# A graph layer on one core: four of 1024 gathers become single row loads, messages are formed in place, edges get four buffers

## The chip, the cores and the metric

The kernel runs on one core of a Trainium2 chip. The metric is device time in microseconds of one execution; the kernel before has a median of 1315.23 us over three runs (1314.40 to 1316.04).

## What is computed

One layer of a graph network on 8192 nodes with 256 channels and 131072 edges, sorted by target, all in float32. Cut to what matters:

```
msg  = relu(x[src] + edge_attr @ w_e + b_e)          # 131072 x 256; edge_attr has 64 columns
t    = x + segment_sum(msg, dst)                     # 8192 x 256
h1   = bn(relu(t @ w1 + b1) @ w2 + b2 + x)           # local branch
h2   = bn(attention(x) @ out_w.T + out_b + x)        # 4 heads within groups of 32 nodes
o    = h1 + h2
o    = bn(o + relu(o @ m_w1 + m_b1) @ m_w2 + m_b2)
out  = layernorm(x + o)
```

## The kernel before

**Tiles.** The edges are cut into 128 blocks of 1024 (`NB`), each with eight gathers of 128 rows: four groups `h` times two tiles `j`. The nodes are cut into 16 chunks of 512. `x + b_e` is written once to a DRAM tensor `xb`; blocks from 20 (`NX`) on gather from it.

**A block's way.** `gather` (L200) issues eight indirect DMAs on POOL (GpSimd) that bring the rows of `x` into a tile `xs`, of which there are four. `load_edges` (L217) brings a block's edge features with four DMAs on SP (SyncE) into `ea`, two buffers; `edge_transpose` (L237) turns them on DVE (VectorE) into `eaT`. `edge_products` (L245) multiplies them with `w_e` on PE (TensorE) into a pair of PSUM banks `pe`, two buffers, which the attention's scores (`pe<-qk` in the profile) use too. `edge_messages` (L269) adds `pe` and `xs` on DVE into a tile `msg`, three buffers, two instructions a block (L281), and applies relu on ACT (ScalarE, L285). `group_sums` (L300) sums messages by target: eight matmuls of a one-hot tile `oh` with `msg` into `pw`, in four column groups of 32. `edge_place` (L335) puts the sums into the node chunk `xT`.

**Node work.** Attention and the dense layers run as generators in pieces of about 1 to 3 us of PE (`Work`, L783). The program asks for so many microseconds of pieces between the steps of two blocks; behind each piece, and behind each call of `edge_messages`, it calls `between` (L233), which runs the functions in the list `spots`.

**Order.** PE runs in the order in which the code is written. Blocks go in pairs up to 104 (`TAIL`), then singly by a planned clock. From block 24 (`NV`) on, DVE and ACT get their order from the scheduler; SP has its order from the scheduler all through. POOL issues the gathers in order. `hold_fetches` (L183) lets gather number n wait for the last PE instruction that the plan has at or before n x 1.254 - 10 us.

Of the kernel before, what the change touches and what calls it, by code (L numbers as in the profile page):

```python
# [9 lines left out]
FP = mybir.dt.float32  # L10
I32 = mybir.dt.int32
AF = mybir.ActivationFunctionType
# [24 lines left out]
TN = CH // P  # L37
GT = P // NPG
NX = 20
ND = 2  # L40
NV = 24
TAIL = 104
# [36 lines left out]
def gnn_kernel(ctx: ExitStack, tc: tile.TileContext, x, src, dst, edge_attr, w, out):  # L79
    nc = tc.nc  # L80

    const = ctx.enter_context(tc.tile_pool(name="const", bufs=1))
    dram = ctx.enter_context(tc.tile_pool(name="dram", bufs=1, space=DRAM))


    srcd = const.tile([P, ND * NH, TJ], I32, name="srcd")
    for b in range(ND):
        for m in range(EQ):
# [20 lines left out]
    xb = dram.tile([N, C], FP, name="xb")  # L109
# [17 lines left out]
    r = 0  # L127
    for v in VECS:
        n = w[v].shape[0] // P
# [17 lines left out]
    epool = fast.enter_context(tc.tile_pool(name="edge", bufs=1))  # L147
# [10 lines left out]
    xs_of, fetches, marks, mark_at, setup = {}, [], [], [0.0, 0], [True]  # L158
# [7 lines left out]
    def matmul(ps, *args, **kw):  # L166

        mark(ps, nc.tensor.matmul(ps, *args, **kw).ins)  # L168
# [14 lines left out]
    def hold_fetches():  # L183

        i = 0
        for n, fetch in enumerate(fetches):
            if n:
                tc.add_manual_dep(
                    fetch, fetches[n - 1].name,
                    mybir.DependencyInfo(mybir.DependencyClass.NoSync, mybir.DependencyReason.DATA), reason="in order",  # L190
                )
            while i < len(marks) and marks[i][0] <= n * 1.254 - AHEAD:
                i += 1
            if i:
                tc.add_manual_dep(
                    fetch, marks[i - 1][2].name,
                    mybir.DependencyInfo(mybir.DependencyClass.Sync, mybir.DependencyReason.DATA), reason="hold",
                )

    def gather(b):  # L200
        xs = epool.tile([P, NH, TJ, C], FP, name="xs", tag="xs", bufs=4)
        for h in range(NH):
            for j in range(TJ):
                idx = srcd[:, b * NH + h, j : j + 1] if b < ND else srci[:, b, h * TJ + j : h * TJ + j + 1]
                fetches.append(
                    nc.gpsimd.indirect_dma_start(  # L206
                        out=xs[:, h, j, :],
                        out_offset=None,
                        in_=x if b < NX else xb[:, :],
                        in_offset=bass.IndirectOffsetOnAxis(ap=idx, axis=0),  # L210
                    ).ins
                )
        xs_of[b] = xs

    ea_of = {}

    def load_edges(b):  # L217

        ea = ea_of[b] = epool.tile([P, QR + NH * EQ * ED], FP, name="ea", tag="ea", bufs=2)
        for j in range(TJ):  # L220
            for i in range(ED // QR):
                p0, c0 = j * ED + i * QR, (1 - i) * QR
                nc.sync.dma_start(
                    ea[p0 : p0 + QR, c0 : c0 + NH * EQ * ED].rearrange("r (g d) -> r g d", g=NH),
                    edge_attr[b * BE : (b + 1) * BE, :].rearrange("(g j r m) d -> j r g (m d)", j=TJ, r=QR, m=EQ)[j],
                )
# [4 lines left out]
    eaT_of, spots = {}, []  # L231

    def between():  # L233
        for do in spots:
            do()

    def edge_transpose(b):  # L237
        ea = ea_of.pop(b)
        eaT = eaT_of[b] = epool.tile([P, NH * EQ, QR], FP, name="eaT", tag="eaT", bufs=2)
        nc.vector.transpose(eaT, ea[:, QR:].rearrange("p (g d) -> p g d", d=ED)[:, :, :QR])  # L240


    pe_of, msg_of, oh_of, pw_of, newest = {}, {}, {}, {}, {}

    def edge_products(b, pairs=range(0, NH, 2)):  # L245

        eaT = eaT_of[b].rearrange("p (h m) r -> p h (m r)", h=NH)
        for h in pairs:
            pe = bank2().rearrange("p i (u c) -> p i u c", u=2)
            half = [slice(i * ED, (i + 1) * ED) for i in range(2)]  # L250
            if b < NX:
                for i, rows in enumerate(half):
# [8 lines left out]
            pe_of[b, h] = pe  # L261

    def next_edges(b):
        if b < NB:
            edge_transpose(b)
        if b + 2 < NB:
            load_edges(b + 2)

    def edge_messages(b, pairs=range(0, NH, 2), of_pair=range(2)):  # L269

        xs = xs_of[b]
        if b not in msg_of:
            msg_of[b] = epool.tile([P, NH, TJ, C], FP, name="msg", tag="msg", bufs=3)
        msg = msg_of[b]
        n = 2 if b < NB - 1 else 1
        for h in pairs:
            pe = pe_of[b, h]
            for u in of_pair[::n]:
                hs = slice(h + u, h + u + n)
                for js in [slice(0, TJ)] if n == 2 or h + u < NH - 1 else [slice(j, j + 1) for j in range(TJ)]:  # L280
                    nc.vector.tensor_add(  # L281
                        msg[:, hs, js].rearrange("p u i c -> p i u c"), pe[:, js, u : u + n, :],
                        xs[:, hs, js].rearrange("p u i c -> p i u c"),
                    )
                    nc.scalar.activation(msg[:, hs, js], msg[:, hs, js], AF.Relu)  # L285
        between()
# [74 lines left out]
    with tc.tile_pool(name="setup", bufs=1) as sp:  # L361
# [9 lines left out]
        load_edges(1)  # L371
        nc.sync.dma_start(be, w["b_e"][None, :].to_broadcast([P, C]))
        nc.sync.dma_start(dsti_r, dst.rearrange("(s e) -> s e", s=NB))
        in_r = npool.tile([P, 3 * KC, C], FP, name="in_r", tag="m1")
        out_r = npool.tile([P, KC, C], FP, name="out_r", tag="vn")
        vec_r = npool.tile([nrows, P], FP, name="vec_r", tag="pr")
        for v in VECS:
            r, n = col[v]
# [474 lines left out]
    with tc.manual_schedule(engines={PE}):  # L853
# [137 lines left out]
        t, l, s = came[b - 2] + 20, b - 2, b - 2  # L991
        p, m = [b, 0], [b, 0]
# [10 lines left out]
        while l < NB:  # L1003
# [56 lines left out]
            elif t >= times[2]:  # L1060
                i, k = p
# [17 lines left out]
    with tc.If(wide > 0):  # L1079
        with tc.tile_pool(name="gen", bufs=1) as pool, tc.tile_pool(name="gen_ps", bufs=1, space=PSUM) as ps_pool:  # L1080
# [11 lines left out]
            with tc.For_i(0, E, P * TE) as e0:  # L1092
                ea = pool.tile([P, TE, ED], FP, name="gea")
# [7 lines left out]
                xs = pool.tile([P, TE, C], FP, name="gxs")  # L1101
# [7 lines left out]
                for j in range(TE):  # L1109
# [89 lines left out]
```

## Time and profile before

| | us |
|---|---|
| median of three runs | 1315.23 |
| profiled execution, its own time | 1313.34 |
| span of the profiled execution | 1311.6 |
| PE busy | 1199.5 (91%) |
| POOL busy | 975.3 (74%) |
| DVE busy | 797.8 (61%) |
| ACT busy | 584.5 (45%) |

The profile is one execution; the span goes from its first instruction to its last. Rows of groups read: line, engine, operation, out<-in, count, busy time and mean of one in ns, then the engine's idle time before these instructions and what ended it. Times in a timeline count from the span's start.

### The profile page before, as it was taken

Reading aid. Unit: us, or ns where it says so; the run is one execution under the profiler, and the core shown is the slowest. Engines: PE = TensorE matmul, PEld = TensorE weight load, DVE = VectorE, ACT = ScalarE, POOL = GpSimd, SP = SyncE. Lnnn points to the kernel's source line nnn. Section 1 sums busy time; section 2 is a strip of 40 time slices with the busy share of each in tenths; the row PEclk is TensorE's granted clock in tenths of the full one; section 3 lists DMA queues with packets and bytes.
Section 4 is the critical chain, followed back from the end, with each engine's and each line's share of the span. In section 5 each row is a group of like instructions: output and inputs, shape, how many; then the busy total and the mean of one; then the engine's idle time right before and its main releaser. Section 6 shows DMA issues by size and latency. Waiting matters only on the chain.

```text
span 1311.6 us, 21687 instructions
## 1 busy us (share of the span) xinstructions
PE 1199.5 (91%) x7671; PEld 723.0 (55%) x7671; DVE 797.8 (61%) x1630; ACT 584.5 (45%) x840; POOL 975.3 (74%) x1032
## 2 busy tenths in 40 slices
PE   4998999998979979899898988989989799999997
PEld 3564556565545555555555555555555555556576
DVE  6676856757447465475745746456474665766563
ACT  2443534545435355253543536435363443545343
POOL 7777777777777777777777777777777777777772
PEclk9998999999979989899998998989999899999999
DMA  9999985767667666666676666666666675756552
GB/s 230 297 307 280 293 230 158 201 160 191 157 159 188 163 185 162 161 184 157 186 169 169 171 165 184 158 169 180 160 185 163 174 189 138 201 154 185 152 152 64
DMA packets 148926, 240.38 MB, mean 183 GB/s; under 512 B 27950, under 2 KB 112204, under 8 KB 148044
## 3 DMA queue, kind: packets, MB, share of 16 engines
q0 software_dynamic: 49152, 134.28, 38.6%
q1 hardware_dynamic: 98572, 104.65, 29.5%
q8 instruction: 62, 1.02, 0.3%
q14 instruction: 52, 0.43, 0.1%
q10 hardware_dynamic: 1088, 0.00, 0.0%
HBM read 222.06 MB, written 16.78 MB: 182 GB/s over the span
## 4 chain that ended last, share of the span: by engine, by line
PE 69%; DMA 10%; DVE 9%; issue 5%; POOL 3%; ACT 2%; SPq 0%; DVEq 0%; POOLq 0%; ACTq 0%
PE at L168 36%; PE pe L168 18%; PE pw L168 7%; DMA xs<-xb,srci 7%; PE l L168 5%; POOL xs L206 3%; DVE msg L281 3%; DMA xs<-in_x_dram,srci 2%; PE at L704 1%; DVE bd L578 1%; PE at L655 1%; DMA xn<-in_x_dram 1%; ACT msg L285 1%; DVE eaT L240 1%; ACT pr L558 1%
## 5 line engine op out<-in xcount | busy, mean ns | idle before, releaser
L206 POOL DMA_INDIRECT xs<-xb,srci x864 | 820.0, 949 | 263.2 <-issue 168.1
L285 ACT ACTIVATE msg<-msg 128x1024 f32<-128x1024 f32 (+1 forms) x259 | 270.7, 1046 | 472.1 <-DVE msg L281 471.0
L281 DVE TENSOR_TENSOR msg<-pe,xs 128x1024 f32<-128x1024 f32 (+1 forms) x259 | 310.2, 1207 | 261.7 <-DMA xs<-xb,srci 172.5
L168 PE MATMUL pe<-we,eaT 64*128 64x256 f32 x2048 | 263.7, 393 | 6.5 <-DVE msg L281 6.3
L168 PEld LDWEIGHTS pe<-we,eaT 64*128 64x128 f32 x2048 | 191.4, 189 | 100.9 <-issue 60.3
L206 POOL DMA_INDIRECT xs<-in_x_dram,srci x144 | 137.7, 956 | 43.9 <-issue 29.9
L168 PE MATMUL pw<-msg,oh 128*32 128x256 f32 x2048 | 136.1, 385 | 1.6 <-ACT msg L285 1.4
L168 PE MATMUL at<-xT,inT 128*128 128x512 f32 x256 | 121.0, 599 | 2.1 <-ACT xT L507 1.7
L168 PE MATMUL at<-hA,mw 128*128 128x512 f32 (+1 forms) x256 | 115.2, 576 | 0.0
L293 DVE TENSOR_TENSOR oh<-iota_n,rel 128x128 f32<-128x128 f32 x256 | 62.1, 279 | 79.8 <-PE pw L168 79.3
L168 PE MATMUL at<-m,mw 128*128 128x512 f32 (+1 forms) x256 | 108.9, 570 | 0.0
L240 DVE STREAM_TRANSPOSE eaT<-ea 128x512 f32<-128x512 f32 x128 | 89.5, 699 | 21.9 <-PE pe L168 18.8
L168 PEld LDWEIGHTS pw<-msg,oh 128*32 128x32 f32 x2048 | 55.1, 109 | 82.9 <-issue 36.7
L168 PE MATMUL pe<-qk 64*128 64x128 f32 x512 | 50.1, 357 | 51.3 <-DVE msg L281 51.3
L168 PE MATMUL l<-oh,ws 128*128 128x160 f32 (+4 forms) x512 | 87.5, 312 | 1.5 <-ACT xT L507 1.5
L168 PEld LDWEIGHTS l<-oh,ws 128*128 128x128 f32 x512 | 76.3, 200 | 22.1 <-issue 16.3
L168 PEld LDWEIGHTS at<-xT,inT 128*128 128x128 f32 x256 | 47.0, 190 | 59.8 <-issue 51.2
L168 PEld LDWEIGHTS pe<-qk 64*128 64x128 f32 x512 | 43.5, 255 | 61.0 <-DVE msg L281 58.0
L168 PEld LDWEIGHTS at<-m,mw 128*128 128x128 f32 x256 | 47.0, 190 | 46.5 <-issue 45.3
L168 PEld LDWEIGHTS at<-hA,mw 128*128 128x128 f32 x256 | 46.5, 191 | 44.6 <-issue 39.8
L352 DVE TENSOR_TENSOR xT<-l,xT 128x352 f32<-128x352 f32 (+14 forms) x107 | 42.8, 422 | 42.0 <-PE l L168 41.8
L636 ACT ACTIVATE m<-at,vec 128x512 f32<-128x512 f32 (+1 forms) x64 | 41.9, 657 | 54.6 <-PE at L168 54.5
(153 smaller groups left out, 1284.6 us busy)
## 6 DMA issues: line engine op xcount, KB each, us to landing
ea<-in_edge_attr_dram SPq DMA_DIRECT2D x512, 128.0 KB
xs<-xb,srci POOLq DMA_INDIRECT x864
xn<-in_x_dram SPq DMA_DIRECT2D x16, 512.0 KB
out_dram<-y SPq DMA_DIRECT2D x14, 512.0 KB
xp<-in_x_dram SPq DMA_DIRECT2D x10, 512.0 KB
xb<-xp SPq DMA_DIRECT2D x10, 512.0 KB
xp<-in_x_dram SPq DMA_DIRECT2D x3, 1024.0 KB
xb<-xp SPq DMA_DIRECT2D x3, 1024.0 KB
```

The lines of the kernel that those rows point to most:

```text
L168: mark(ps, nc.tensor.matmul(ps, *args, **kw).ins)
L206: nc.gpsimd.indirect_dma_start(out=xs[:, h, j, :], out_offset=None, in_=x if b < NX else xb[:, :], in_offset=bass.IndirectOffsetOnAxis(ap= ...
L240: nc.vector.transpose(eaT, ea[:, QR:].rearrange("p (g d) -> p g d", d=ED)[:, :, :QR])
L281: nc.vector.tensor_add(msg[:, hs, js].rearrange("p u i c -> p i u c"), pe[:, js, u : u + n, :], xs[:, hs, js].rearrange("p u i c -> p i u c"),
L285: nc.scalar.activation(msg[:, hs, js], msg[:, hs, js], AF.Relu)
L293: nc.vector.tensor_tensor(oh[:, ts], iota_n[:, None, :WN].to_broadcast([P, TB // 2, WN]), rel[:, b, ts, None].to_broadcast([P, TB // 2, WN ...
L352: newest["xT"] = nc.vector.tensor_add(xT, l2[:, :, a - n : z - n], xT).ins
L558: nc.scalar.copy(pr[q, :, 2 * hh : 2 * hh + 2, :].rearrange("p t s k -> p s t k"), two4[q, :, :, q])
L578: nc.vector.transpose(bd[q, :, :, g, :].rearrange("p t h q -> p (t h) q"), pr3[q])
L636: newest["relu"] = nc.scalar.activation(m1[:, o, :], layer(mw1, KC, o, hA), AF.Relu, bias=v_("m_b1", o)).ins
L655: nc.tensor.transpose(ps[:wt, t - t2, k * P : (k + 1) * P], zT[:, k, t * P : t * P + wt], ident)
L704: nc.tensor.matmul(ps[i], wt[:, k, o * P : (o + 1) * P], act[:, k, :], start=(k == 0), stop=(k == nk - 1))
```

## The change

- Blocks 46, 62, 78 and 94 (`FETCHED`) issue seven gathers instead of eight. The 128 rows of the last one are loaded by SP into a tile `xf` (two buffers), one DMA of 1 KB for each row. `row_stream` makes pieces of four rows: one load of four row numbers from `last_src` into SP registers, then four DMAs with a register's address.
- From block 26 (`FROM`) on each block gives leave for two pieces (`RUN`), eight rows; `some_rows`, a new function in `spots`, issues one piece where there is leave. 128 pieces take 64 blocks.
- `ea` has four buffers instead of two. `next_edges` loads two blocks ahead up to its block 24, then three, and four from 26.
- Messages are formed in place: `msg` is the tile `xs`, which has six buffers (`BUFS`).
- In the four blocks the last pair's add is three instructions: both groups' first tiles, then the second tile from `xs`, then the one from `xf`.
- A fetch keeps the number that it would have had, so the holds use the same plan as before.

```diff
+BUFS = 6
+RUN = 2
+FETCHED = [46, 62, 78, 94]
+FROM = 26
...
     def gather(b):
-        xs = epool.tile([P, NH, TJ, C], FP, name="xs", tag="xs", bufs=4)
+        xs = epool.tile([P, NH, TJ, C], FP, name="xs", tag="xs", bufs=BUFS)
         for h in range(NH):
             for j in range(TJ):
+                if b in FETCHED and h * TJ + j == TB - 1:
+                    continue
...
-                fetches.append(
+                fetches.append((
+                    b * TB + h * TJ + j,
...
+    def row_stream():
+
+        for b in FETCHED:
+            xf = xf_of[b] = epool.tile([P, C], FP, name="xf", tag="xf", bufs=2)
+            for r in range(QR):
+                _, rows = nc.values_load_multi_w_load_instructions(
+                    last_src[b : b + 1, r * EQ : (r + 1) * EQ], engines=[mybir.EngineType.SP], min_val=0, max_val=N - 1,
+                    skip_runtime_bounds_check_because="src holds rows of x, as for the gathers",
                 )
+                for m, row in enumerate(rows):
+                    nc.sync.dma_start(xf[m * QR + r : m * QR + r + 1, :], xb[ds(row, 1), :])
+                yield
...
+    def fetch_rows(b):
+        quota[0] += RUN if b >= FROM else 0
+
+    def some_rows():
+        if quota[0]:
+            quota[0] -= 1
+            next(rows_to_come, None)
...
-        ea = ea_of[b] = epool.tile([P, QR + NH * EQ * ED], FP, name="ea", tag="ea", bufs=2)
+        ea = ea_of[b] = epool.tile([P, QR + NH * EQ * ED], FP, name="ea", tag="ea", bufs=4)
...
-        if b + 2 < NB:
-            load_edges(b + 2)
+        ahead = 2 + (b >= 24) + (b >= 26)
+        while loaded[0] < min(b + ahead, NB - 1):
+            loaded[0] += 1
+            load_edges(loaded[0])
+        fetch_rows(b - 2)
...
-            msg_of[b] = epool.tile([P, NH, TJ, C], FP, name="msg", tag="msg", bufs=3)
+            msg_of[b] = xs
...
+                if h + u + n == NH and b in FETCHED:
+                    for us, js, rows in (
+                        (slice(0, 2), slice(0, TJ - 1), xs[:, h:]), (slice(0, 1), slice(TJ - 1, TJ), xs[:, h:]),
+                        (slice(1, 2), slice(TJ - 1, TJ), xf_of[b]),
+                    ):
+                        rows = rows[:, None, None, :] if rows is xf_of[b] else rows[:, us, js].rearrange("p u i c -> p i u c")
+                        nc.vector.tensor_add(
+                            msg[:, h:][:, us, js].rearrange("p u i c -> p i u c"), pe[:, js, us, :], rows
+                        )
+                    nc.scalar.activation(msg[:, hs], msg[:, hs], AF.Relu)
+                    continue
...
+        nc.sync.dma_start(last_src, src.rearrange("(s e) -> s e", s=NB)[:, BE - P :])
...
+        spots.append(some_rows)
```

The order of instructions on PE is the same but for the tile's name; what differs is what they wait for. Here PE's sums of one block in the tail are shown with the semaphores that each row waits for, first before, then in the change (`pw` sums, `oh` one-hot tile, DMASW a gather's semaphore).

```order
L168 MATMUL at<-m_6942,mw_95 128x512 x3
L168 MATMUL pw<-msg,oh 32x256 [waits DVE_49,Activation_49]
L168 MATMUL pw<-msg,oh 32x256
L168 MATMUL pw<-msg,oh 32x256 [waits DVE_49]
L168 MATMUL pw<-msg,oh 32x256 x5
```
```order
L172 MATMUL pw<-xs,oh 32x256 [waits DMASW7_49,Activation_49]
L172 MATMUL pw<-xs,oh 32x256 [waits DMASW1_49]
L172 MATMUL pw<-xs,oh 32x256 [waits DMASW3_49,Activation_49]
L172 MATMUL pw<-xs,oh 32x256 [waits DMASW5_49]
L172 MATMUL pw<-xs,oh 32x256 [waits DMASW0_49]
L172 MATMUL pw<-xs,oh 32x256 [waits DMASW2_49]
L172 MATMUL pw<-xs,oh 32x256 [waits DMASW4_49]
L172 MATMUL pw<-xs,oh 32x256 [waits DMASW6_49]
```

Every matmul of a group now waits for a gather by itself, and each also counts up PE's semaphore by itself instead of one for all eight.

On SP, in the part from block 26 on, before: edge loads (`ea`), a chunk's nodes (`xn`) and an output store.

```order
L223 DMA ea<-in_edge_attr_dram 32x4x256 x32
L359 DMA xn<-in_x_dram 128x4x256
L678 DMA out_dram<-y 128x4x256
L223 DMA ea<-in_edge_attr_dram 32x4x256 x32
L359 DMA xn<-in_x_dram 128x4x256
```

And the change, near one such node load (`TENSOR_LOAD last_src` reads four row numbers, `ISA` works out an address, `xf` is a row):

```order
L259 DMA ea<-in_edge_attr_dram 32x4x256 x4
L411 DMA xn<-in_x_dram 128x4x256
L232 TENSOR_LOAD last_src
L237 ISA
L237 DMA xf<-xb 1x256
L237 ISA
L237 DMA xf<-xb 1x256
L731 DMA out_dram<-y 128x4x256
```

Rows stand between all other transfers of SP, also ahead of and behind the store.

On DVE at block 46, before (`msg` adds, `sm` and `pr` softmax, `bd` its turned weights, `eaT` turned edges):

```order
L281 TENSOR_TENSOR msg<-pe,xs 128x2x2x256
L571 TENSOR_REDUCE sm<-pr 128x16
L281 TENSOR_TENSOR msg<-pe,xs 128x2x2x256
L572 RECIPROCAL sm<-sm 128x16
L240 STREAM_TRANSPOSE eaT<-ea 128x512
L574 TENSOR_TENSOR pr<-pr,sm 128x128 x4
```

And in the change:

```order
L333 TENSOR_TENSOR xs<-pe,xs 128x2x2x256
L624 TENSOR_REDUCE sm<-pr 128x16
L327 TENSOR_TENSOR xs<-pe,xs 128x2x256
L625 RECIPROCAL sm<-sm 128x16
L327 TENSOR_TENSOR xs<-pe,xs 128x256
L627 TENSOR_TENSOR pr<-pr,sm 128x128 x4
L327 TENSOR_TENSOR xs<-pe,xf 128x256
L631 STREAM_TRANSPOSE bd<-pr 32x16x32 x4
L276 STREAM_TRANSPOSE eaT<-ea 128x512
```

The second add is cut in three, with softmax steps between its parts, and the edges of a later block are turned behind them. The other three blocks look alike.

More of the change, by code (lines that the diff above doesn't have):

```diff
@@ L185, in hold_fetches @@
         i = 0
-        for n, fetch in enumerate(fetches):
-            if n:
+        former = None
+        for n, fetch in fetches:
+            if former:
                 tc.add_manual_dep(
-                    fetch, fetches[n - 1].name,
+                    fetch, former.name,
                     mybir.DependencyInfo(mybir.DependencyClass.NoSync, mybir.DependencyReason.DATA), reason="in order",
@@ L193, in hold_fetches @@
                 i += 1
+            former = fetch
             if i:
@@ L210, in gather @@
                         in_offset=bass.IndirectOffsetOnAxis(ap=idx, axis=0),
-                    ).ins
-                )
-        xs_of[b] = xs
+                    ).ins,
+                ))
+        xs_of[b] = xs
+    last_src = const.tile([P, P], I32, name="last_src")
+    xf_of = {}
+    def row_stream():
[5 more added lines that the diff above has]
+                    skip_runtime_bounds_check_because="src holds rows of x, as for the gathers",
+                )
+                for m, row in enumerate(rows):
+                    nc.sync.dma_start(xf[m * QR + r : m * QR + r + 1, :], xb[ds(row, 1), :])
+                yield
+    rows_to_come = row_stream()
+    quota = [0]
+    def fetch_rows(b):
[4 more added lines that the diff above has]
+            next(rows_to_come, None)
     ea_of = {}
     def load_edges(b):
-        ea = ea_of[b] = epool.tile([P, QR + NH * EQ * ED], FP, name="ea", tag="ea", bufs=2)
+        ea = ea_of[b] = epool.tile([P, QR + NH * EQ * ED], FP, name="ea", tag="ea", bufs=4)
         for j in range(TJ):
@@ L261, in edge_products @@
             pe_of[b, h] = pe
+    loaded = [3]
     def next_edges(b):
```

## The prediction

> **What bounds the kernel now.** I read the page first: the span, the busy shares, the group of the gathers and the shares of the chain that ended last.
>
> ```profile
> span 1311.6 us, 21687 instructions
> PE 1199.5 (91%) x7671; PEld 723.0 (55%) x7671; DVE 797.8 (61%) x1630; ACT 584.5 (45%) x840; POOL 975.3 (74%) x1032
> ...
> PE 69%; DMA 10%; DVE 9%; issue 5%; POOL 3%; ACT 2%; SPq 0%; DVEq 0%; POOLq 0%; ACTq 0%
> ...
> L206 POOL DMA_INDIRECT xs<-xb,srci x864 | 820.0, 949 | 263.2 <-issue 168.1
> ```
>
> PE is busiest and carries 69% of the chain, so the first guess is that PE is the bound. POOL looks free for a quarter of the time. The second view corrects this: POOL's timeline, two neighbouring gathers, and the instructions of line 206 with their first and last start.
>
> ```profile
> 607.00 0.95 POOL L206 DMA_INDIRECT xs<-xb,srci  x1 [0.30 <-issue]
> 608.25 0.94 POOL L206 DMA_INDIRECT xs<-xb,srci  x1 [0.30 <-issue]
> ...
> ```
> ```profile
> L206 POOL DMA_INDIRECT xs<-xb,srci x864: 942/946/1442, 207.4 to 1289.4; - x173
> ...
> L206 POOL DMA_INDIRECT xs<-in_x_dram,srcd x16: 942/946/1701, 4.4 to 24.6; - x16
> ```
>
> A gather is 0.95 us busy and 0.30 us pause, 1.25 us from start to start. All 1024 start between 4.4 and 1289.4: 1285.0 / 1023 = 1.256 us each. So POOL issues gathers without a break from beginning to end, and its 26% "idle" is the pause that every gather has. What POOL waits for confirms it:
>
> ```profile
> POOL xs L206 <- issue: 205.0, 665, 2.8
> POOL xs L206 <- PE at L168: 25.3, 83, 0.3
> POOL xs L206 <- DMA xs<-xb,srci: 22.9, 75, 0.3
> ```
>
> The waits on other engines are never over 0.3 us, the same pause: neither a full buffer nor the holds of `hold_fetches` stop it. Now who waits for the gathers? The waits between 1000 and 1080 us, then the group that stands there, over the whole run, and PE's busy time in three stretches.
>
> ```profile
> DVE msg L281 <- DMA xs<-xb,srci: 16.9, 7, 4.1
> ...
> PE pe L168 <- DVE msg L281: 7.0, 2, 3.8
> ```
> ```profile
> L168 PE MATMUL pe<-qk 64*128 64x128 f32 x512 | 50.1, 357 | 51.3 <-DVE msg L281 51.3
> ```
> ```profile
> 1025.00:1034.50 9.50, 2.45 (x21) 1.92 (x19) 2.56 (x3) 1.13 (x2) 7.37 (x8) 0.69 0.59 154
> ...
> 1085.00:1217.00 132.00, 129.08 (x828) 77.62 (x832) 85.46 (x172) 63.89 (x98) 100.01 (x106) 0.99 0.64 169
> ```
> ```profile
> 1120.00:1290.00 170.00, 167.35 (x1098) 105.73 (x1097) 109.00 (x236) 79.75 (x128) 128.87 (x136) 1.00 0.62 166
> ```
>
> In a stretch's row the first number behind the length is PE's busy time. Around 1030 PE stands for 7.0 us, because the add that frees its bank waits for a gather: up to there the gathers set the pace and PE follows. The score matmuls (`pe<-qk`) stand like this for 51.3 us in all. Behind that PE is busy 129.1 of 132 us and 167.4 of 170 us: in the last 250 us PE is nearly full, and its chain touches the gathers only here:
>
> ```profile
> 1078.60 4.25 DMA xs<-xb,srci
> 1082.97 1.24 DVE msg L281
> 1084.23 1.06 ACT msg L285
> 1085.34 1.06 PE pw L168 x12
> ...
> 1217.68 0.34 POOL xs L206
> ...
> 1218.99 4.30 DMA xs<-xb,srci
> ```
>
> So two things must come earlier together: the gathers, and PE's start into its full stretch.
>
> **The change, part by part.** *Four gathers go.* Each takes one slot: 4 x 1.256 = 5.02 us by which the POOL stream ends earlier (1.25 after block 46, 5.02 after block 94, whose gathers end at 95 x 8 x 1.256 = 955 us). What is late next is PE. At 1025 it follows gathers that come 5.02 us earlier instead of 3.77 (what the three before gave, taken up at earlier stands of the same kind), so it needs 1.25 us more out of a stand of 7.0 us. From there its full stretch starts 5.0 us earlier, the gathers at 1078 and 1218 come 5.0 us earlier too, and the order of PE's instructions is the same. The gain is 5.0 us. It can't be much more: both contacts with the stream at 1078 and 1218 cap it.
>
> *The holds.* A held gather waits for a PE instruction that the plan puts 10 us behind it, and the plan's numbers are the same (a skipped gather keeps its number). If PE comes forward as the gathers do, holds cost nothing, as now; if it doesn't, they give the gain back. This is the same condition as above.
>
> *Six buffers in place of four and three.* A gather now waits for the sums of the block six before it, instead of an add of the block four before. In the chain above the sums (1085.34) follow the add at 1082.97, which follows a gather that POOL issued at 1078. In the paired part sums come up to two blocks (20 us) behind the gathers of their pair; six buffers leave more than 20 us of the 60. Cost 0, between 0 and 0.3 us a gather if a wait landed in the pause; I take 0, as the quoted waits are all inside the pause. The adds lose a wait for a message buffer; no such wait stands among the long ones, gain 0.
>
> *Waits and counts on PE.* The sums now read a tile that gathers write and that a later gather overwrites, so each of the eight matmuls of a group carries a wait of its own (see the order above) and tells its end by itself. The trace has groups with one to three waits, not with eight. Two groups, and the number of PE records of `pw` behind 1083 us (16 a group: 22 groups):
>
> ```profile
> 1120.77 1.07 PE L168 MATMUL pw<-msg,oh 128*32 128x256 f32 x16
> ...
> 1128.87 1.07 PE L168 MATMUL pw<-msg,oh 128*32 128x256 f32 x16
> ```
> ```profile
> 1083.00:1312.00 229.00, 24.89 (x352) 9.73 (x352) 8.20 (x22) 0.99 0.55 149
> ```
> ```profile
> L168 PEld LDWEIGHTS pw<-msg,oh x2048: 106/110/118, 47.3 to 1295.0; 128*32 128x32 f32 x187
> ```
>
> Both take 1.07 us, though waits sit on their first and third matmuls. Lower end 0 (nothing is taken off PE). Upper end: seven more waits at a weight load each, the nearest row of the same queue, 7 x 0.11 = 0.77 us, and 22 x 0.77 = 17 us. I take 0, nearest to the two equal groups; 17 us is kept for the range. The Trainium skill, "TensorE: Matmul & The Clock Gate", section "The cost: per-tile semaphore tail", speaks against the change here: increments on every tile's matmul serialize, at about 26 ns each. By it seven more are an estimated 0.18 us a group, 4 us over 22 groups, and the sum would be 1.0 us instead of 5.0; no run here shows it yet.
>
> *ACT.* Each relu now has two extra waits for gathers in front. The nearest row is ACT's own semaphore instruction.
>
> ```profile
> L328 ACTq EVENT_SEMAPHORE  x18: 17/17/17, 1072.2 to 1287.4; - x18
> ```
>
> Two for each of 259 relus, 518 x 0.017 = 9 us on an engine that is 45% busy, and they wait for what the add has already waited for: 0 on the path.
>
> *The adds of the four blocks.* Their last pair is three instructions in place of one.
>
> ```profile
> L281 DVE TENSOR_TENSOR msg<-pe,xs 128x1024 f32<-128x1024 f32 x254 | 307.4, 1219 | 258.8 <-DMA xs<-xb,srci 169.6 <-PE pe L168 58.3 <-issue 9.0
> ...
> L281 DVE TENSOR_TENSOR msg<-pe,xs 128x512 f32<-128x512 f32 x3 | 2.1, 691 | 2.9 <-DMA xs<-xb,srci 2.9
> ...
> L281 DVE TENSOR_TENSOR msg<-pe,xs 128x256 f32<-128x256 f32 x2 | 0.7, 415 | 0.0
> ```
>
> 0.69 + 2 x 0.42 = 1.52 against 1.22 us: +0.30 us x 4, and the softmax's steps now stand between the parts. All four lie before 1025, where the stand of 7.0 us absorbs it. Cost 0; without that cover 1.2 us.
>
> *SP.* 512 single rows, 128 register loads, four buffers of edges. What SP waits for between 470 and 960 us, and the price of its instructions:
>
> ```profile
> SPq L223 <- DVE eaT L240: 290.8, 42, 8.6
> SPq L223 <- DVE oh L293: 48.6, 7, 8.1
> SPq L678 <- DVE y L673: 32.6, 6, 6.6
> SPq L359 <- DVE st L663: 22.7, 7, 4.9
> ```
> ```profile
> L379 SPq DMA_DIRECT2D vec_r<-in_L_gnn_bn_g_dram x3: 231/232/252, 12.3 to 17.7; - x3
> ```
> ```profile
> L223 SPq DMA_DIRECT2D ea<-in_edge_attr_dram x512: 311/432/1758, 3.4 to 1247.3; - x171
> ```
> ```profile
> L1078 SPq TENSOR_LOAD <-width x1: 536/536/536, 1308.3 to 1308.3; - x1
> ```
>
> SP waits 394.7 of 490 us, 8.06 us of each block's 10.0. Added per block: 2 x 0.54 + 8 x 0.23 (a load of 1 KB, like a row) = 2.9 us, at 0.43 a row 4.5 us. It fits into the waiting. Behind a row in the queue stand the next edges, node loads and stores; edges now have two more buffers, 20 us of cover. The rows of a block are fetched some four blocks before its add. Cost 0.
>
> **Sum.** The profiled execution took 1313.34 us, 1.7 us around its span of 1311.6. 1313.3 - 5.0 = 1308.3. The median shown, 1315.23, lies 1.9 us above that execution; the runs after will be set beside such a median, so 1315.2 - 5.0 = **1310.2 us**.
>
> **The rivals.** *The groups of sums grow.* Should seven more counts lengthen a group by 0.11 to 0.21 us (10 to 20% of 1.07), 22 groups take 2.4 to 4.6 us of PE's full stretch, and the gain is 2.6 to 0.4: 1312.6 to 1314.8. Against it: the two equal groups. For it: PE has nothing to spare behind 1085. The skill's rule above is this case, at its middle. Chance 0.18.
>
> *The other side: the sums lose their overlap.* Four column groups run at once: 16 passes of 0.379 us (their median in line 168's rows) in 1.07 us.
>
> ```profile
> L168 PE MATMUL pw<-msg,oh x2048: 379/379/412, 47.3 to 1295.2; 128*32 128x256 f32 x187
> ```
>
> If a wait or a count on every matmul breaks the overlap in part, PE loses more than the 5 us; it decides from 5.0 / 22 = 0.23 us a group, and is past 0.2% slower from 0.35. At the upper end of 0.77 the stretch grows by 17 us: 1327; with no overlap at all (16 x 0.379 = 6.1 us) far more. Chance 0.08.
>
> *SP becomes the bound.* From (8.06 - 1.07) / 8 = 0.87 us a row edges fall behind. The longest edge issue, 1.76 us, would make a block 7 us too long; over the 64 blocks from 26 on, less 20 us of cover, more than 400 us. The medians 0.23 and 0.43 speak against it. Chance 0.06. The Trainium skill, "DMA: Bandwidth & Descriptors", section "Anatomy of one DMA — SWDGE (gpsimd) path", gives each DMA a fixed 2 us, which would be 16 us for eight rows, an estimate; the edge issues at 0.43 us, in fours, show that it isn't paid one after another.
>
> *The change doesn't do what it says.* POOL gets the four slots back, but the rows' transfers slow other gathers by as much: 5.0 / 500 = 10 ns a gather is enough. POOL's step is 1.25 us beside SP's bursts of edges as well as without. Then 1315. Chance 0.08.
>
> **How the numbers follow.** Forecast 0.60, 1308.5 to 1311.8; groups grow 0.18; nothing gained 0.08; slower 0.14 (0.08 + 0.06). A measurement of this kernel can tell about 0.2%, 2.6 us, from no change: faster below 1312.6, slower above 1317.9. Faster 0.60, same 0.26, slower 0.14. The range goes from 1308.0 to 1316.5: the forecast and nearly all of the two middle cases; what is left out is the slower 0.14 and a small rest.
>
> **What would show it.** In the profile after: 1020 gathers at 1.25 us, the last starting near 1284.4; the stand around 1025 near 5.8 us; `pw` groups of 1.07 us; PE's stretch behind it as full as now; SP's rows at 0.23 to 0.45 us with waits left. It is wrong if the `pw` groups last over 1.2 us, if POOL shows waits over 0.3 us, or if PE waits for transposed edges.

## The result and the profile after

The change takes 1310.12 us (median of 7 runs, 1309.59 to 1312.61) against 1315.23 before (7 runs): ratio 0.9966, 95% interval 0.9956 to 0.9976. That is 5.1 us less. Ratios and intervals here are taken over all runs of both kernels, so they differ a little from the quotient of two medians. A repeat on another chip of the same speed gave 1310.50 against 1315.45, 0.9959 [0.9946, 0.9973]. Two further chips took 1557 us for the kernel before, and what ran there is compared only with the kernel before on the same chip.

The page of the change, with the rows that answer to those shown of before:

```profile
span 1307.8 us, 23877 instructions
PE 1199.0 (92%) x7671; PEld 720.0 (55%) x7671; DVE 799.4 (61%) x1638; ACT 585.9 (45%) x840; POOL 972.6 (74%) x1028
...
L215 POOL DMA_INDIRECT xs<-xb,srci x860 | 817.1, 950 | 262.0 <-issue 173.7
```

No engine does noticeably less or more, but for POOL, 2.7 us less; 2190 instructions more are in the program. The place of the 5 us can't be seen on this page. The instructions of the gathers' line and what POOL waits for:

```profile
L215 POOL DMA_INDIRECT xs<-xb,srci x860: 942/946/1736, 207.6 to 1285.5; - x172
...
L215 POOL DMA_INDIRECT xs<-in_x_dram,srcd x16: 942/946/1386, 4.3 to 24.1; - x16
```
```profile
POOL xs L215 <- issue: 209.6, 680, 2.7
POOL xs L215 <- PE at L172: 20.4, 67, 0.3
```

1020 gathers from 4.3 to 1285.5 are 1281.2 / 1019 = 1.257 us each: the same stream, four slots shorter, still never held by another engine for over 0.3 us. Its last gather starts 3.9 us earlier than in the profile of before (1289.4), not 5.0: beyond 1.25 us a step, before has 1285.0 - 1023 x 1.25 = 6.2 us and after 1281.2 - 1019 x 1.25 = 7.4 us of irregular steps. The profiled executions differ by 3.8 us (1313.34 and 1309.59), the medians by 5.1.

Where PE gets ahead is seen at landmarks in its timeline. First before: the two groups of scores at which it stood, the next node transposes, a group of sums that waits for its messages, later node transposes, and the last dense group.

```profile
1029.09 2.08 PE L168 MATMUL pe<-qk 64*128 64x128 f32 x16 [3.77 <-DVE msg L281]
1034.44 2.08 PE L168 MATMUL pe<-qk 64*128 64x128 f32 x16 [3.28 <-DVE msg L281]
...
1048.03 1.04 PE L172 MATMUL at<-ident,xn 128*128 128x128 f32 x8
...
1085.34 1.06 PE L168 MATMUL pw<-msg,oh 128*32 128x256 f32 x12 [1.44 <-ACT msg L285]
...
1125.98 1.04 PE L172 MATMUL at<-ident,xn 128*128 128x128 f32 x8
...
1304.21 1.89 PE L737 MATMUL pe<-mw,m 128*128 128x256 f32 x8
```

The same places after (in brackets what PE stood for):

```profile
1025.53 1.80 PE L172 MATMUL pe<-qk 64*128 64x128 f32 x16 [2.48 <-DVE xs L333]
1029.13 2.08 PE L172 MATMUL pe<-qk 64*128 64x128 f32 x16 [1.81 <-DVE xs L333]
...
1042.28 1.04 PE L176 MATMUL at<-ident,xn 128*128 128x128 f32 x8
...
1071.21 1.14 PE L172 MATMUL pe<-we,eaT 64*128 64x256 f32 x8 [1.47 <-DVE xs L333]
...
1122.76 1.04 PE L176 MATMUL at<-ident,xn 128*128 128x128 f32 x8
...
1300.52 1.89 PE L790 MATMUL pe<-mw,m 128*128 128x256 f32 x8
```

PE restarts 5.3 us earlier after its stand (1034.44 to 1029.13), has 5.75 us at 1042, and gives 2.5 us of it back by 1122.76, with a new wait at 1071 for an add that waits for gathers. From there to the end the difference stays between 3.2 and 3.7 us.

Not all of the 5.3 us comes from the four slots. The restart hangs on one gather, in the chains (start, time until it has landed) first before, then after:

```profile
1028.57 4.47 DMA xs<-xb,srci
```
```profile
1024.87 2.86 DMA xs<-xb,srci
```

Both times the scores start 1.40 us behind its landing (1033.04 and 1027.73). It was issued 3.7 us earlier, which is the stream, and it landed 1.6 us sooner after that, which the slots don't explain: such a gather at the restart also landed in 2.73 and 2.78 us in two kernels without a gain (without rows, and with late slots, below). The next contact takes the 1.6 us back:

```profile
1074.96 4.64 DMA xs<-xb,srci
...
1082.10 1.06 PE pw L172 x12
```

The group of sums at 1082.10 is the one that stood at 1085.34 before, behind the gather of 1078.60. That gather is issued 3.64 us earlier now and takes 0.39 us longer to land, so the sums start 3.24 us earlier, and with this lead PE goes on. PE's rows of the later stretches, and `pw` alone from there to the end (22 groups, as before):

```profile
1085.00:1217.00 132.00, 129.40 (x816) 77.03 (x815) 85.64 (x172) 63.64 (x97) 100.00 (x106) 0.99 0.65 171
```
```profile
1075.00:1308.00 233.00, 25.29 (x352) 9.84 (x352) 8.20 (x22) 0.99 0.54 146
```

PE is as full as before (129.4 of 132 us), and 22 groups take 25.29 us instead of 24.89, 0.02 us a group more. That this comes from the eight waits and counts is not shown: the kernel with the rows alone, below, whose sums wait as before, takes 27.08 us for 23 groups, 0.03 us a group more than the change.

### The profile page after: what moved, and what is told of

Same layout as the page of the kernel before. It is cut to its first block, busy times and chain, and to the rows that moved or that the text cites. A ratio compares the mean times of both kernels' runs of the same rounds, so it can differ in the third digit from the quotient of the medians.

```text
span 1307.8 us, 23877 instructions
## 1 busy us (share of the span) xinstructions
PE 1199.0 (92%) x7671; PEld 720.0 (55%) x7671; DVE 799.4 (61%) x1638; ACT 585.9 (45%) x840; POOL 972.6 (74%) x1028
## 4 chain that ended last, share of the span: by engine, by line
PE 71%; DMA 10%; DVE 7%; issue 6%; POOL 4%; ACT 2%; SPq 1%; DVEq 0%; POOLq 0%; ACTq 0%
PE at L172 36%; PE pe L172 19%; PE pw L172 8%; DMA xs<-xb,srci 7%; PE l L172 4%; POOL xs L215 4%; DVE xs L333 3%; PE at L757 1%; DMA xn<-in_x_dram 1%; ACT xs L337 1%; DMA xs<-in_x_dram,srci 1%; PE at L708 1%; DVE bd L631 1%; PE at L176 1%; DMA ea<-in_edge_attr_dram 0%
## 5 line engine op out<-in xcount | busy, mean ns | idle before, releaser
L337 ACT ACTIVATE xs<-xs 128x1024 f32<-128x1024 f32 (+1 forms) x255 | 266.5, 1046 | 441.6 <-DVE xs L333 405.8
L333 DVE TENSOR_TENSOR xs<-pe,xs 128x1024 f32<-128x1024 f32 (+1 forms) x255 | 304.7, 1208 | 230.9 <-DMA xs<-xb,srci 142.5
L172 PE MATMUL pw<-xs,oh 128*32 128x256 f32 x2048 | 136.5, 385 | 3.0 <-ACT xs L337 2.3
L172 PE MATMUL at<-hA,mw 128*128 128x512 f32 (+1 forms) x256 | 118.6, 591 | 0.2 <-ACT xT L560 0.2
L276 DVE STREAM_TRANSPOSE eaT<-ea 128x512 f32<-128x512 f32 x128 | 89.8, 702 | 22.3 <-PE pe L172 20.2
L172 PEld LDWEIGHTS pw<-xs,oh 128*32 128x32 f32 x2048 | 55.2, 109 | 84.5 <-issue 36.9
L172 PE MATMUL pe<-qk 64*128 64x128 f32 x512 | 45.8, 336 | 39.7 <-DVE xs L333 39.7
L172 PEld LDWEIGHTS pe<-qk 64*128 64x128 f32 x512 | 39.7, 235 | 48.9 <-DVE xs L333 46.1
```

What stands on the lines that cost most here:

```text
L333: nc.vector.tensor_add(msg[:, hs, js].rearrange("p u i c -> p i u c"), pe[:, js, u : u + n, :], xs[:, hs, js].rearrange("p u i c -> p i u c"),
```

## The experiments

### Buffers, messages in place and waits, without rows

```diff
-FETCHED = [46, 62, 78, 94]
+FETCHED = []
```

> All of the change but the rows: 1024 gathers, messages in place in six buffers, four buffers of edges, a wait and a count on each matmul of the sums. If the four slots of POOL are the whole gain: 1315.2 us (1314 to 1316.5), the last gather starts near 1289, PE stands 7 us around 1025. If in-place messages or the edge buffers carry part of the gain: 1310 to 1313. If the waits and counts on the sums cost PE 0.1 us or more a group: 1317.5 or more.

Measured: 1315.60 (11 runs) against 1315.27 (23 runs), 0.9995 [0.9986, 1.0005]. All 1024 gathers are on POOL, and everything else of the change is in. So six buffers, messages in place, ACT's extra waits and eight waits and counts for each group of sums together lie between a loss of 0.7 us and a gain of 1.8 us. PE's stand in this profile, over 1000 to 1080 us, is smaller than the 7.0 us of before:

```profile
PE pe L172 <- DVE xs L333: 5.1, 2, 3.7
```

The two kernels take the same time with stands of 7.0 and 5.1 us, so a difference of 2 us in this stand, between two profiles, says nothing. The restart moves too: it is at 1035.73 us here, 1.3 us later than before.

### Rows without the new buffers

```diff
-        xs = ... bufs=BUFS)
+        xs = ... bufs=4)
-        ea = ... bufs=4)
+        ea = ... bufs=2)
-        ahead = 2 + (b >= 24) + (b >= 26)
+        ahead = 2
-            msg_of[b] = xs
+            msg_of[b] = epool.tile([P, NH, TJ, C], FP, name="msg", tag="msg", bufs=3)
```

> The rows without the buffers: four gathers replaced by row loads, but two buffers of edges, four of gathered rows, three of messages as before the change. If the slots are the whole gain and SP's queue has room: 1310.2 us (1309 to 1311.5). If the rows make edges late unless they have more buffers: 1312 or more, with PE waiting for transposed edges.

Measured: 1312.15 (7 runs), 0.9975 [0.9964, 0.9986]: 3.1 us gained, some 2 less than by the whole change; the two intervals overlap, so the two aren't told apart. The expectation named transposed edges as what PE would wait for; it was something else. What PE waits for between 470 and 960 us has a row here that neither the kernel before nor the change has, and PE's timeline shows its longest case:

```profile
PE at L176 <- DMA xn<-in_x_dram: 11.5, 3, 7.1
```
```profile
897.86 1.97 PE L176 MATMUL at<-ident,xn 128*128 128x128 f32 x8 [7.05 <-DMA xn<-in_x_dram]
```

SP's timeline tells why: first this kernel, then the change.

```profile
872.05 3.88 SPq L237 DMA_DIRECT2D xf<-xb  x8
886.30 1.76 SPq L259 DMA_DIRECT2D ea<-in_edge_attr_dram  x4
888.81 3.93 SPq L237 DMA_DIRECT2D xf<-xb  x8
893.13 0.40 SPq L411 DMA_DIRECT2D xn<-in_x_dram  x1
```
```profile
877.64 0.41 SPq L411 DMA_DIRECT2D xn<-in_x_dram  x1
```

Two edge buffers make the edge load of 886.30 wait 10.3 us in SP's queue, until DVE has turned the edges before it (`SPq L259 <- DVE eaT L276`), with eight rows and the node chunk `xn` behind it; PE stood from 890.8 on. With four buffers `xn` is issued at 877.64. In this profile the 11.5 us are won back before the stand at 1029: there PE waits for gathers again and restarts at 1032.77, behind a gather issued at 1028.28. This is 3.4 us later than in the change, but POOL was never held by another engine for over 0.3 us; its stream had 12.1 us of irregular steps in this execution, against 7.4. So whether the waits for `xn` cost the median anything is not shown.

### Six blocks instead of four

```diff
-RUN = 2
-FETCHED = [46, 62, 78, 94]
+RUN = 3
+FETCHED = [40, 51, 62, 73, 84, 95]
```

> Six blocks with row loads (40, 51, 62, 73, 84, 95), twelve rows a block. If each slot gives 1.256 us as long as PE can come forward at a stand of 7 us: 1315.2 - 7.5 = 1307.7 us (1306.5 to 1309). If PE's full stretch caps the gain near the 5 us of four: 1310. If SP falls behind with twelve rows a block: over 1312.

Measured: 1309.61 (5 runs), 0.9952 [0.9938, 0.9966]. That is 6.3 us (4.5 to 8.2) below before. The median lies above the 1306.5 to 1309 expected for six slots and near the 1310 expected for a cap, but the interval of the gain holds both 7.5 us and the change's 5.1, so neither is shown. Its PE comes out of the stand another 1.0 us earlier and then meets the gathers at the same place, where the sums stand for 2.5 us:

```profile
1028.09 2.08 PE L172 MATMUL pe<-qk 64*128 64x128 f32 x16 [3.78 <-DVE xs L333]
...
1081.06 1.45 PE L172 MATMUL pw<-xs,oh 128*32 128x256 f32 x12 [2.48 <-ACT xs L337]
```

Its last gather starts at 1285.0, hardly before the 1285.5 of the change: 1280.7 - 1017 x 1.25 = 9.5 us of irregular steps have eaten most of the two further slots in this execution. SP still waits, but less (its longest wait for edge buffers):

```profile
SPq L259 <- DVE eaT L276: 27.3, 7, 8.2
```

With its three other waits (24.4, 9.8 and 7.8 us) that is 69 of the 490 us between 470 and 960, against 196 us in the change:

```profile
SPq L259 <- DVE eaT L276: 86.5, 25, 8.3
SPq L259 <- DVE oh L345: 69.8, 18, 6.4
SPq L731 <- DVE y L726: 25.8, 6, 5.5
SPq L411 <- DVE st L716: 13.5, 6, 3.9
```

### The rows loaded and gathered too

```diff
-                if b in FETCHED and h * TJ + j == TB - 1:
-                    continue
```

> The four blocks load the last 128 rows singly and gather them too; the add takes the singly loaded ones. So all 1024 gathers and all the row traffic. If rows cost nothing where they run: 1315.2 us (1314 to 1316.5). If the 512 small transfers slow the gathers: POOL's step grows above 1.256 us on average between 300 and 950 us and the time is 1317 or more.

Measured: 1316.24 (11 runs), 1.0005 [0.9996, 1.0014]. With all 1024 gathers on POOL the rows, their register loads and the four split adds cost 1.0 us by the medians, between a gain of 0.5 and a loss of 1.8 us by the interval. So the rows' transfers don't slow the other gathers by 10 ns each, which would be 5 us, and what the change gains comes from the four missing slots. The rows aren't free on PE, though: between 470 and 960 us it waits 10.9 us for ACT's copies of a node chunk (`xT`) here and 11.4 us in the change, against 6.4 us before and in the kernel without rows. The stands for gathers further on take these 5 us up; what makes ACT late was not tried.

### Four slots behind the last stand

```diff
-RUN = 2
-FETCHED = [46, 62, 78, 94]
+RUN = 0
+FETCHED = [106, 110, 114, 118]
...
-    xf_of = {}
+    xf = const.tile([P, C], FP, name="xf")
+    nc.vector.memset(xf, 0.0)
+    xf_of = {b: xf for b in FETCHED}
...
-        ea = ... bufs=4)
+        ea = ... bufs=3)
-        ahead = 2 + (b >= 24) + (b >= 26)
+        ahead = 2 + (b >= 24)
```

> The late blocks (106, 110, 114, 118) without the rows: POOL leaves the four gathers out, SP loads no row, and the four adds take zeros in their place (128 rows of each of the four blocks are left out of the messages). Built to be read on either sort of chip. Where the kernel before takes about 1315: theory (behind PE's last stand a slot is worth nothing) 1314.9 (1314.2 to 1316.0), with PE's stands between 1020 and 1035 as long as before; rival (POOL's stream is the bound up to the end) 1310.2. Where the kernel before takes about 1557, as on the chips of the last six runs: there the kernel with these four gathers and the rows took 1574 to 1578. If the 512 rows and 128 register loads on SP are what cost the 17 to 21 us there, this one takes 1551 to 1558; if buffers and messages in place cost them, 1573 to 1580.

Beside it, on the same chip, the change itself:

> The change itself as a control beside the other run. Where the kernel before takes about 1315: 1310.1 (1309.0 to 1311.2). Where it takes about 1557: between 1570 and 1580, a ratio of 1.008 to 1.015, as the three kernels there with the same 512 rows had 1.011 to 1.014, wherever their four blocks lay and whichever buffers they had; a ratio below 1.000 would say that the late blocks and the fewer buffers were what cost the time there.

Measured: 1314.59 (11 runs), 0.9995 [0.9986, 1.0004], and the change 1310.50 (5 runs), 0.9959 [0.9946, 0.9973], with 1315.45 (15 runs) for before. Four gathers fewer, and at most 1.8 us gained. No rows are loaded here either: zeros stand in for the 512 rows, which are left out of the messages. The first gather left out is the one that the chain of before meets at 1078.60 (number 106 x 8 + 7 = 855), and all four lie ahead of the one at 1218. The gathers' lines of the two, the late one first:

```profile
L215 POOL DMA_INDIRECT xs<-xb,srci x860: 942/946/1392, 209.9 to 1286.1; - x172
```
```profile
L215 POOL DMA_INDIRECT xs<-xb,srci x860: 942/946/1759, 207.8 to 1286.2; - x172
```

POOL issues its last gather at the same moment in both. PE's second scores and its last dense group don't lie at the same moment, again the late one first:

```profile
1034.38 2.08 PE L172 MATMUL pe<-qk 64*128 64x128 f32 x16 [2.47 <-DVE xs L335]
...
1304.00 1.89 PE L792 MATMUL pe<-mw,m 128*128 128x256 f32 x8
```
```profile
1029.13 2.08 PE L172 MATMUL pe<-qk 64*128 64x128 f32 x16 [1.98 <-DVE xs L333]
...
1301.44 1.89 PE L790 MATMUL pe<-mw,m 128*128 128x256 f32 x8
```

The late kernel restarts where before did (1034.44), and its end stays there. That the two restarts agree to 0.1 us is chance: the late one's gather was issued 1.6 us later (1030.20) and landed in 2.78 us instead of 4.47. What carries the argument is the medians: four slots ahead of the stand gain 4.95 us, four behind it at most 1.8, with POOL done at the same moment. So the time is not set by when POOL is done, but by when PE comes into its full stretch.

### Six runs on the slower chips

The late blocks with their rows (ea three buffers, xf four), twice:

> The change with the four blocks moved to the end: 106, 110, 114 and 118 instead of 46, 62, 78 and 94, all behind PE's last stand around 1025 us (xf has four buffers and ea three, since the rows now lie ready for longer). POOL issues four gathers fewer here too. Theory (gathers set the pace only up to PE's last stand; behind it PE is full, so a slot given back there is given to nobody): no gain from the slots, 1314.9 (1314.2 to 1316.0), with PE's stand before 1035 as long as before (about 7 us in all). Rival (POOL's stream is the bound up to the end): 1310.2, as in the change.

> The late blocks (106, 110, 114, 118) once more, since the chip of the last four runs took 1557 us for the kernel before, with pauses on all engines, and can't be set beside the others. Where the kernel before takes about 1315 us: theory (behind PE's last stand a slot is worth nothing) 1314.9 (1314.2 to 1316.0), with about 7 us of stands of PE between 1020 and 1035; rival (POOL's stream is the bound up to the end) 1310.2. Where the kernel before is again far above 1315, only the ratio to the change's other kernels on that chip can be read.

Eight blocks:

```diff
-RUN = 2
-FETCHED = [46, 62, 78, 94]
+RUN = 4
+FETCHED = [40, 48, 57, 66, 74, 83, 91, 100]
```

> The change with eight blocks instead of four (40, 48, 57, 66, 74, 83, 91, 100), four pieces of rows for each block. Theory (a slot is worth 1.256 us as long as PE can come forward): eight slots are 10.0 us, but PE's stand after the six-block kernel was only 3.8 us in its profile, so about two more slots are taken up and then PE is full: 1306 to 1308. Rival (SP is the bound now: 15 rows of 0.29 us, nearly four register loads of 0.56 us and the edges' 1.7 us are about 8.3 of a block's 10 us, so node chunks and stores come late and PE stands for them, as it did for the node transposes in the kernel with rows alone): 1310 to 1314, with SP's waits between 470 and 960 us below 60 us and PE standing before at<-ident,xn.

The change with two edge buffers (`bufs=2`, `ahead = 2`), twice:

> The change with the two edge buffers of before (ea bufs 2, two blocks ahead); messages in place in six buffers and all rows as in the change. The kernel with rows alone was about 2 us slower than the change and its PE stood for a chunk's nodes that SP loaded late behind edges that had no free buffer. Theory (the four edge buffers are what keeps SP's queue moving): 1312.2 (1311.3 to 1313.3) and PE stands before at<-ident,xn again. Rival (the six buffers in place are what matters): 1310.2 and no such stand.

> The change with the two edge buffers of before, once more, for the same reason. Theory (four edge buffers keep SP's queue moving): 1312.2 (1311.3 to 1313.3), and PE stands before at<-ident,xn for a node chunk. Rival (the six buffers in place are what matters): 1310.2 and no such stand. On the slow chip PE did stand there, 18.7 us in three waits for xn.

The change with four edge buffers, but gathered rows in four buffers and messages of their own:

```diff
-        xs = ... bufs=BUFS)
+        xs = ... bufs=4)
-            msg_of[b] = xs
+            msg_of[b] = epool.tile([P, NH, TJ, C], FP, name="msg", tag="msg", bufs=2)
```

> The other half: rows and four edge buffers as in the change, but four buffers of gathered rows and messages in tiles of their own (two of them, since three don't fit). Theory (the edge buffers matter, the messages' place doesn't): 1310.2 (1309.0 to 1311.5), no stand before at<-ident,xn. Rival (the six buffers in place matter): 1312.2. Should two message buffers in place of three hold up the adds by themselves, DVE's waits on PE before the adds show it.

Measured, with before at 1557.32 (11 runs) on one chip and 1557.38 (11 runs) on the other:

| | us | ratio to before |
|---|---|---|
| late blocks | 1574.21 | 1.0112 [1.0082, 1.0142] |
| late blocks, again | 1577.91 | 1.0123 [1.0085, 1.0161] |
| eight blocks | 1680.54 | 1.0799 [1.0758, 1.0841] |
| two edge buffers | 1579.47 | 1.0138 [1.0109, 1.0167] |
| two edge buffers, again | 1578.94 | 1.0131 [1.0095, 1.0168] |
| edges alone | 1574.45 | 1.0119 [1.0083, 1.0155] |

On these chips PE makes pauses for which the profile names no engine, and POOL waits for PE. What PE and POOL wait for in the first late run:

```profile
PE pw L172 <- issue: 45.9, 61, 2.5
```
```profile
POOL xs L215 <- PE pw L172: 53.7, 43, 3.5
```

In the change, on a chip of 1315 us, PE has no wait put down to `issue`, and POOL waits for no other engine over 0.3 us. The times expected for 1315 us therefore say nothing here. Two things can be read. First, which buffers keep `xn` coming. With two edge buffers PE stood for it in both runs (first, then again):

```profile
PE at L176 <- DMA xn<-in_x_dram: 18.7, 3, 9.0
```
```profile
PE at L176 <- DMA xn<-in_x_dram: 22.6, 3, 10.8
```

With four edge buffers and messages of their own, and with three in the late blocks, there is no such row. So the edge buffers do it, not the messages' place; that agrees with the kernel with rows alone. What this is worth in time, the ratios don't tell: their intervals overlap. Second, what happens when SP is full. With eight blocks the two longest waits of SP between 470 and 960 us, and PE's longest of the whole run:

```profile
SPq L237 <- DMA xf<-xb: 8.9, 19, 1.4
SPq L259 <- DVE oh L345: 1.8, 1, 1.8
```
```profile
PE at L176 <- DMA xn<-in_x_dram: 132.0, 7, 22.1
```

SP waits 11 of 490 us, PE waits 132 us for node chunks, and the kernel is 123 us slower than before on that chip: the rival "SP becomes the bound", seen at twice the rows on a chip with pauses. Why the five kernels with 512 rows took 17 to 22 us more than before on those chips stays open: no trace of before was taken there, and neither the change as it stands nor a kernel without rows ran there. Eight blocks on a chip of 1315 us weren't tried either.

## Why the prediction was right, point by point

**POOL sets the pace and PE is full behind 1034 us: right.** The late slots bear it out: the gathers end at 1286.1 as in the change, and at most 1.8 us is gained. "Not at the end of POOL's stream" was the choice that mattered, and it would have been easy to make the other.

**Four slots, 5.02 us: right within the interval.** 5.1 and 4.95 us in the medians; the first interval allows 3.2 to 5.8 us, so the agreement with 5.0 to a tenth of a microsecond is luck. Counted against the kernel that loads the rows and gathers them too, it is 1.0005 - 0.9966 = 0.0039, also 5.1 us.

**"The gathers at 1078 and 1218 cap it": right at 1078, loose at 1218.** PE had 5.75 us at 1042, more than the stream gave in that profile, and lost 2.5 us by 1123, with its waits at 1071 and 1082 for gathers; the six blocks met the same place. The second contact, at 1218, is not on the chain of the first profile, which follows no gather behind 1110, but it is on the chain of the repeat:

```profile
1215.85 4.69 DMA xs<-xb,srci
```

There the gather comes 3.1 us earlier than before, and this execution is 2.8 us shorter than the profiled one of before. The late slots relieve this contact and gain at most 1.8 us. That "the gathers come 5.0 us earlier" is not what single profiles show: 3.64 us at 1078 in the first, 3.1 us at 1218 in the repeat, since the irregular steps differ.

**The stand near 5.8 us: not confirmed.** 2.48 + 1.81 = 4.3 us at the two groups of scores, 4.1 in the repeat (2.12 and 1.98). But kernels of equal time have 7.0 and 5.1 us there, and the late one 4.8, so this term was asked of a number that varies by 2 us for other reasons. The restart tells more, but it isn't sharp either: 1029.13 twice with the gain, and 1034.44, 1034.38, 1035.73 and 1036.83 without it (before, the late slots, no rows, rows and gathers).

**The last gather near 1284.4: 1.1 us off.** It started at 1285.5. The mean step of 1.256 us held (1.257), but a few irregular steps, not the same ones in every execution, move the end by a microsecond or more.

**Holds and six buffers, cost 0: right.** POOL's waits on others stay at 0.3 us in the change, and all of it together, without rows, is 0.9995 [0.9986, 1.0005]. In two other kernels with messages in place, the one with rows and gathers and the late one, POOL waits once for PE's sums (2.1 and 2.0 us, at 150.96 us).

**Waits and counts on every matmul of the sums, cost 0: right.** The kernel without rows has these waits and counts, and lies at most 0.7 us above before. "The groups of sums grow" (2.4 to 4.6 us) and "the sums lose their overlap" (over 5 us) are both out. The Trainium skill, "TensorE: Matmul & The Clock Gate", section "The cost: per-tile semaphore tail", let the prediction expect an estimated 4 us over the 22 groups, at 26 ns for each count. The delay is there, but behind PE and smaller than 0.18 us a group: it shows in when ACT copies a finished group (`ws`), first before, then in the change.

```profile
1147.98 1.07 PE L168 MATMUL pw<-msg,oh 128*32 128x256 f32 x16
1149.17 0.37 ACT L328 COPY ws<-pw 128x256 f32<-128x256 f32 x1 [0.40 <-PE pw L168]
```
```profile
1144.76 1.07 PE L172 MATMUL pw<-xs,oh 128*32 128x256 f32 x16
1146.03 0.37 ACT L380 COPY ws<-pw 128x256 f32<-128x256 f32 x1 [0.47 <-PE pw L172]
```

The copy starts 0.12 us behind the sums before and 0.20 us in the change. Among the some 20 copies in each profile that wait for PE, the usual delay is 0.12 us where a group counts once (before, and the rows alone) and 0.20 us in the six profiles with messages in place on chips of 1315 us. The further 0.08 us are three times 26 ns; that would be the four matmuls that end a group together, whose counts queue, while the four before them are long done. No run separates this. PE goes on with other matmuls meanwhile.

**ACT's waits and the split adds, cost 0: right together.** ACT has 505 of these waits, with a median of 38 ns instead of the 17 taken. Neither was tried alone; the first is in the kernel without rows, both in the one with rows and gathers (1.0005).

**SP has room: right, but nearer to its limit than it looked, and not without the edge buffers.** Priced at 0.23 to 0.43 us a row and 0.54 us a register load; the rows' instructions:

```profile
L237 SPq DMA_DIRECT2D xf<-xb x512: 224/228/350, 183.8 to 918.7; - x171
```
```profile
L232 SPq TENSOR_LOAD <-last_src x128: 468/562/1573, 183.0 to 916.6; - x128
```

Eight rows with the register load between them last 3.88 us in the timeline above, so a row is (3.88 - 0.56) / 8 = 0.41 us, at the upper end. The Trainium skill, "DMA: Bandwidth & Descriptors", section "Anatomy of one DMA — SWDGE (gpsimd) path", has its fixed 2 us for DMAs that GpSimd issues; these rows go out from SyncE, and at 0.41 us a row they don't pay it one after another. 394.7 us of waiting became 196, 4.1 us a block, inside the 2.9 to 4.5 us of the prediction. What the prediction left out: "the rows fit into the waiting" holds for the sum, but SP is a queue, and where an edge load waits for its buffer, rows and `xn` wait behind it. The prediction took the two further edge buffers as 20 us of cover and counted no gain for them; without the new buffers PE did wait for `xn`, but a loss in time, 3.1 against 5.1 us gained, is not told apart.

**The rows slow other gathers: out at the 10 ns that the rival needs.** 1.0005 [0.9996, 1.0014] with both.

## What to carry to other kernels

An engine that issues without a break sets the time only up to the last place where the bound engine waits for it: here four slots ahead of that place were worth 5 us, and four behind it at most 1.8, though the stream ended just as early. Read such a gain from the medians; in a single profile follow the chain to the transfer on which the bound engine restarts, and split its lead into issue and landing, before you trust the stand's length or the restart. Work moved onto a queue in order delays what waits behind its head, so give the head (here the edge loads) buffers before the queue gets more to do.

## What the runs showed of the hardware

- An indirect gather of 128 rows of 1 KB takes POOL one step of 1.25 us; single steps are longer, 6.2 to 12.1 us in all over some 1020 gathers in the eight profiles on chips of 1315 us. The steps over 1.5 us between 390 and 1000 us lie within 4 us of 402, 482, 560, 641, 720 or 802 us in all of them, but not all in each.
- Four gathers on which PE's restart hung landed 2.73, 2.78, 2.86 and 4.47 us after their issue (no rows, late slots, the change, before): 1.7 us that no slot explains.
- ACT's copy of a group of sums starts mostly 0.20 us behind the group's last matmul where all eight matmuls count up PE's semaphore, and 0.12 us where one does.
- A row of 1 KB with its address in a register takes SP 0.228 us for the DMA, and loading four addresses 0.56 us; eight rows last 3.88 us with the load between them and 4.4 us with both loads. The 128 rows that replace one step of 1.25 us on POOL are 16 x 4.4 = 70 us of SP: cheap only on a queue that has nothing else to do.
- The same program took 1315 us on some chips and 1557 us on others, with pauses of PE in the profiles taken there (118.6 us put down to `issue` in the first late run) that no engine explains. The mean granted clock of the kernel before was 0.92 to 0.93 on the latter and 0.96 on the former; that is 4%, not the 18% of the time. A verdict on the first need not hold on the second: the kernels with 512 rows that ran there lost 1.1 to 1.4%, and the change with two edge buffers is among them; the change itself wasn't tried there.
